# Moving the second attention's exp into a step of its own, and spreading the first attention's reciprocals half by half

## The chip, the cores and the metric

The kernel runs on one NeuronCore of one Trainium2 chip. The metric is the device time of one execution in microseconds. Before the change three runs took 3222.53, 3224.51 and 3226.42 us, with a median of 3224.51 us. The profile comes from another execution of the same program, which took 3221.87 us; the span of its instructions is 3220.1 us.

## The reference

Two layers on an image batch `x` of shape (2, 256, 64, 64), all in 32-bit floats.

Layer 0 is full attention over the 4096 pixels of each image, with 8 heads of 32 channels, followed by a 1x1 convolution and a blend by a resized mask:

```python
q = proj(Wq, bq) / math.sqrt(hd); k = proj(Wk, bk); v = proj(Wv, bv)
attn = softmax(einsum('bnd,bmd->bnm', q, k), axis=-1)
fuse = einsum('bnm,bmd->bnd', attn, v)
hybrid = conv1x1(concatenate([x, fuse], axis=1), Wf, bf)
x = hybrid * m + x * (1.0 - m)
```

Layer 1 has a channel gate, attention inside windows of 8 x 8 pixels with 4 heads of 64 channels, and then two grouped 7 x 7 convolutions with normalisation, whose result gates `x`:

```python
x = x * sigmoid(relu(xp @ ca_w1 + ca_b1) @ ca_w2 + ca_b2)
attn = softmax(einsum('whqd,whkd->whqk', q, k) * hd ** (-0.5), axis=-1)   # second attention
o = einsum('whqk,whkd->whqd', attn, v) @ out_w + out_b
x = x + o; x = channel shuffle of x in 4 groups
y = bn2(conv7x7(relu(bn1(conv7x7(x, sa_w1) + sa_b1)), sa_w2) + sa_b2)
return x * sigmoid(y)
```

## The kernel before

A first part (about 210 us) computes queries, keys and values of layer 0 for both images, writes them to DRAM, and prepares the weights of the convolutions. It also decides whether the scores are small enough for a softmax without a shift; with the inputs used they are, and the version of the main part without the shift (its tiles have an `a` in the name) runs.

The main part is a pipeline of 1024 slots. A slot is one image `b` (2), one chunk `c` of 512 query pixels (8 per image), one group `g` of four heads (2), and one block `m` of 128 keys (32). So a pair (b, c) takes 64 slots. In this document the 16 pairs are chunks 0 to 15, and a slot's place inside its chunk is its position, 0 to 63; positions 0 to 31 are the first half (g = 0), 32 to 63 the second.

The order of instructions on every engine is written out by hand: no scheduler reorders them[...]. In slot i, the loop at the end of `pipeline` issues:

- `scores(i + 2)`: four matmuls (L593), one for each head on its own 32 rows of the array, into four PSUM banks, and the exp of these banks on ACT (L603) into an `e` tile. There are five `e` tiles in rotation (`EB = 5`).
- `products(i)`: four matmuls (L622) that add values times `e` into the accumulator `av`; and on DVE the running sum of the `e` tiles over the keys (L624, 128 x 2048 elements), from the half's second slot on. An `e` tile is free once both have read it.
- `run_later()`: the actions put off by `at(delay, action)`. At the end of each chunk these make the reciprocals of the softmax denominators: `denominators` (L645, on PE, reads the two running sums of the chunk), a reciprocal (L673, DVE), `spread` (L659, matmuls that copy each head's reciprocal to the 32 rows of its channels, and two copies L667 on ACT), and the multiplication of the attention's result `f` (L675, DVE). Seen from the next chunk these fall on positions 1, 2, 3 and 4.
- `run_stages()`, in every fourth slot: one step of the generator `stage(b, c)`, which does everything from the 1x1 convolution of layer 0 to the output of the second attention for the chunk before. Its steps end at each `yield`. At positions 8, 12, ..., 52 it issues: the 1x1 convolution `hy` (L693), the two matmuls of the channel gate (L722, L736), queries and keys of the second attention (L762, two steps), its values (L780), the step with its scores (L799) and softmax (L807 to L811), the row sums and division (L814 to L816), the transposes (L824), the products (L837), the output projection (L857), and the addition into `xo` (L868) with its stores `xs` (L883).
- `run_convs()`, in every fourth slot two slots later: one step of `convolve`, which does the two convolutions of an image once its last stage is through: in turn conv1 (L936), conv2 (L959) and gate with the output stores (L981, L990). Image 0's convolution runs beside chunks 8 to 11; image 1's runs after all slots.

[...] One is the accumulator's. While no convolution is under way, the others form two pairs (`psum2`) and three single banks (`psum1`); a slot's scores take one pair and two singles. While one is under way, there are three pairs and one single, and a slot's scores take two pairs. Denominators, spread, stages and conv2 take pairs from the same rotation, conv1 takes a single. A pair is given out again when its last reader is done.

In the step with the second attention's scores and softmax, the queue order is: matmuls on PE; a copy from PSUM on ACT (L807); maximum (L809) and subtraction (L810) on DVE; exp on ACT (L811). It falls on position 32, the first slot of a half, which has no running sum.

Of the kernel before, what the change touches and what calls it, by code (L numbers as in the profile page):

```python
# [19 lines left out]
P = 128  # L20
KC = C // P
# [32 lines left out]
def conv_seq_kernel(ctx: ExitStack, tc: tile.TileContext, a, out):  # L54
    nc = tc.nc
# [13 lines left out]
    def psum2(name):  # L69
        return ps["pair"].tile([P, 2, CH], F32, tag="s", name=name)  # L70
# [41 lines left out]
    for u in range(4):  # L112
        t = const.tile([P, len(BLOCKS), UG, WP], F32, name=f"xc{u}")
        nc.gpsimd.memset(t, 0.0)
        xcs.append(t)
        t = const.tile([P, UQ, len(BLOCKS), WP], F32, name=f"yc{u}")
# [77 lines left out]
    with (  # L194
# [9 lines left out]
        for n in ("bq", "bk"):  # L204
            t = w0.tile([P, KC], F32, name=n)
# [8 lines left out]
        for b in range(B):  # L214
            src = a["x"][b].rearrange("(k p) h w -> p k (h w)", p=P)
            for c in range(NCHUNK):
# [3 lines left out]
                for n, w in (("q", wq), ("k", wk)):  # L220
# [13 lines left out]
                    t = st0.tile([P, KC, CH], F32, tag=n, name=f"{n}st_{b}_{c}")  # L234
# [37 lines left out]
                i = b * NCHUNK + c  # L272
# [36 lines left out]
    def batch_norm(name, t):  # L309
        g, beta, mean, var, cbias = (t[:, :, i] for i in range(5))  # L310
        sc, sh = (cwp.tile(list(g.shape), F32, name=name + i) for i in ("_sc", "_sh"))
        nc.vector.tensor_scalar_add(sc, var, EPS)
        nc.scalar.activation(sc, sc, AF.Sqrt)
        nc.vector.reciprocal(sc, sc)
        nc.vector.tensor_mul(sc, sc, g)
        nc.vector.tensor_sub(sh, cbias, mean)
        nc.vector.tensor_mul(sh, sh, sc)
        nc.vector.tensor_add(sh, sh, beta)
        return sc, sh
# [30 lines left out]
    _, shj = batch_norm("bj", bj)  # L350
# [65 lines left out]
    def spread(row, n):  # L416
        f = row.shape[-1]
        return row.rearrange("p u f -> u p f").to_broadcast([NU, n, f])
# [58 lines left out]
    def pipeline(arm, shifted, pools):  # L477
# [6 lines left out]
        def psum_for(convolving):  # L484
            if convolving != few[0]:
                few[0] = convolving
                name = f"{arm}{now[0]}"
                psum_layout(name, *((3, 1) if convolving else (2, 3)))
# [12 lines left out]
        stages = deque()  # L501
# [3 lines left out]
        def at(delay, action):  # L505
            later.append((now[0] + delay, action))

        def load_piece(n):
            if n * PB >= len(slots):
                return  # L510
            b, c, g, m = slots[n * PB]
            p = m // PB
            nm_ = f"{arm}_{b}_{c}_{g}_{p}"
            k = kvp.tile([P, PB * P], F32, tag="k", name=f"k{nm_}")
            nc.sync.dma_start(k, k_s[b, g, p])
            v = kvp.tile([P, PB, P], F32, tag="v", name=f"v{nm_}")
            nc.sync.dma_start(v, v_s[b, g, p].rearrange("p (m d) -> p m d", m=PB))
            kts[b, c, g, p], vts[b, c, g, p] = k, v

        def load_q(b, c):  # L520
            q = qp.tile([P, KC, CH], F32, tag="q", name=f"q{arm}_{b}_{c}")
            nc.sync.dma_start(q, q_s[b, c].rearrange("p (g n) -> p g n", g=KC))
            qts[b, c] = q
# [87 lines left out]
        def products(i):  # L611
            b, c, g, m = slots[i]
            if m == 0:
                acc[0] = avp.tile([P, CH], F32, tag="av", name=f"av{arm}_{i}")
                acc[1] = ep.tile([P, HG, CH], F32, tag="sum", name=f"sum{arm}_{i}", bufs=3)
                totals[b, c, g] = acc[1]
            av, total = acc[0], acc[1]
            e, v = es[i], vts[b, c, g, m // PB]
            start, stop = m == 0, m == NMB - 1
            for j in range(HG):  # L620
                r = slice(32 * j, 32 * j + 32)
                nc.tensor.matmul(av[r, :], v[:, m % PB, r], e[:, j, :], start=start, stop=stop)  # L622
            if m > 0:
                nc.vector.tensor_add(total, first[0] if m == 1 else total, e)  # L624
            e = es.pop(i)
            if start:
                first[0] = e
            if stop:
                if g == 0:
                    fts[b, c] = fp.tile([P, KC, CH], F32, tag="f", name=f"f{arm}_{b}_{c}")  # L630
                f = fts[b, c]
                nc.scalar.copy(f[:, g, :], av)  # L632
                if g == 0:
                    return
                both = [totals.pop((b, c, gg)) for gg in range(KC)]
                inv = fp.tile([P, P], F32, tag="inv", name=f"inv{arm}_{i}")
                rd = fp.tile([P, KC, 4, P], F32, tag="rd", name=f"rd{arm}_{i}")


                def denominators():  # L640
                    s = psum2(f"dn{arm}_{i}")
                    for h in range(HEADS0):
                        for q in range(4):
                            r = slice(32 * q, 32 * q + 32)
                            nc.tensor.matmul(  # L645
                                s[r, 0, 0:P],
                                keysum[:, h].rearrange("p i h -> p (i h)"),
                                both[h // HG][:, h % HG, q * P : (q + 1) * P],
                                start=(h == 0),
                                stop=(h == HEADS0 - 1),  # L650
                            )
                    nc.scalar.copy(inv, s[:, 0, 0:P])

                def spread():
                    tiles = [psum2(f"rd{arm}_{i}_{hh}") for hh in range(2)]
                    for gg in range(KC):
                        for q in range(4):
                            r = slice(32 * q, 32 * q + 32)
                            nc.tensor.matmul(  # L659
                                tiles[q // 2][:, q % 2, gg * P : gg * P + P],  # L660
                                spread_h[r, gg].rearrange("p j d -> p (j d)"),
                                inv[r, :],
                                start=True,
                                stop=True,
                            )
                    for hh in range(2):
                        nc.scalar.copy(  # L667
                            rd[:, :, 2 * hh : 2 * hh + 2, :],
                            tiles[hh][:, :, 0 : KC * P].rearrange("p q (g n) -> p g q n", g=KC),
                        )  # L670

                at(2, denominators)
                at(3, lambda: nc.vector.reciprocal(inv, inv))  # L673
                at(4, spread)
                at(5, lambda: nc.vector.tensor_mul(f, f, rd.rearrange("p g q n -> p g (q n)")))  # L675


        def stage(b, c):
            x, f = xts.pop((b, c)), fts.pop((b, c))
# [8 lines left out]
            t = gp.tile([P, KC, CH], F32, tag="t", name=f"t{tag}")  # L688
# [44 lines left out]
            for oc in range(KC):  # L733
                for h in range(2):
                    r = slice(64 * h, 64 * h + 64)
# [7 lines left out]
            t = gp.tile([P, KC, CH], F32, tag="t", name=f"sg{tag}")  # L743
# [13 lines left out]
            for h in range(2):  # L757
# [11 lines left out]
                for j in range(KC):  # L769
                    n = 2 * h + j  # L770
# [21 lines left out]
            for hc in range(2):  # L792
                for t in range(4):
                    for w in range(2):
                        for h in range(2):
                            r = slice(64 * h, 64 * h + 64)
# [11 lines left out]
            mx = gp.tile([P, 16], F32, tag="mxw", name=f"mxw{tag}")  # L808
            nc.vector.tensor_reduce(mx, e, AX.X, ALU.max)  # L809
            nc.vector.tensor_sub(e, e, mx.unsqueeze(2).to_broadcast([P, 16, 64]))  # L810
            nc.scalar.activation(e, e, AF.Exp, scale=HD1**-0.5)  # L811
            yield
            rs = gp.tile([P, 16], F32, tag="rsw", name=f"rsw{tag}")
# [7 lines left out]
            for n in range(16):  # L821
                for w in range(2):
                    r = slice(64 * w, 64 * w + 64)
# [7 lines left out]
            for hc in range(2):  # L831
                for t in range(4):
                    for w in range(2):
                        for h in range(2):
                            n = 2 * hc + h
                            r = slice(64 * w, 64 * w + 64)
# [30 lines left out]
            for oc in range(KC):  # L867
# [5 lines left out]
                for n, (x0, _, _) in enumerate(BLOCKS):  # L873
# [4 lines left out]
                    for h in range(2):  # L878
                        q = 2 * oc + h
                        p = 32 * q + 1 - x0  # L880
# [135 lines left out]
        def run_later():  # L1016
            for _ in range(len(later)):
                due, action = later.popleft()
                if due <= now[0]:
                    action()  # L1020
                else:
                    later.append((due, action))
# [15 lines left out]
        for i, (b, c, g, m) in enumerate(slots):  # L1038
            now[0] = i
            psum_for(bool(convs))  # L1040
            if m % PB == 0:
                load_piece(i // PB + AHEAD)
            if g == KC - 1 and m == 0:
                nxt = (b, c + 1) if c + 1 < NCHUNK else (b + 1, 0)
                if nxt[0] < B:
                    load_q(*nxt)
            rest = scores(i + 2) if i + 2 < len(slots) else None
            products(i)
            if rest:
                rest()  # L1050
            if g == KC - 1 and m == NMB - 1:
                at(6, lambda b=b, c=c: stages.append(stage(b, c)))
            run_later()
            if i % 2:
                next(banded, None)
            if i % 4 == 0:
                run_stages()
            if i % 4 == 2:
                run_convs()
# [94 lines left out]
```

## Time and profile before

| engine | busy, us | share of the span |
|---|---|---|
| PE (matmul) | 3110.8 | 97% |
| DVE | 2553.6 | 79% |
| ACT | 2377.1 | 74% |
| POOL | 400.9 | 12% |

| part of a plain slot | time, us |
|---|---|
| L593, eight matmul records together | 1.14 |
| L622, eight matmul records together | 1.06 |
| L603, the exps of four banks | about 2.0 |
| L624, running sum | 2.29 |

An engine's share of busy time is an average over the whole span. A matmul of 32-bit floats leaves two records in the profile, and the records of matmuls on different rows of the array overlap. In lists of waits, the engine that waits is on the left and what ended the wait on the right, followed by the total in us, how often, and the longest. In the timeline a line is a start, a duration, the engine, the source line and the tiles; in square brackets stands the idle time of that engine just before, with what ended it. In tables of stretches each engine has its busy time and, in brackets, its number of instructions; PEclk is the clock granted to PE as a share of the full one.

### The profile page before, as it was taken

What the parts mean: (1) busy time and instruction counts of PE and PEld (TensorE: products, weight loads), DVE (VectorE), ACT (ScalarE), POOL (GpSimd) and SP (SyncE); (2) the same over time, 40 slices, a digit from 0 to 9 for tenths busy, and PEclk for the clock granted to TensorE, in tenths of its full rate; (3) what the DMA queues carried; (4) which work ended last, traced back from release to release, by engine and by line L of the source; (5) the groups of instructions that cost most, each with busy time, mean ns of one, the idle gap of its engine ahead of it and who ended that gap; (6) DMA issues with size and microseconds to landing.
All of it is one profiled execution on the core that took longest, in us unless ns stands there. A gap on an engine that the chain in (4) does not pass through costs nothing. (4 is left out here: it accounts for less than half of the span.)

```text
span 3220.1 us, 62227 instructions
## 1 busy us (share of the span) xinstructions
PE 3110.8 (97%) x26122; PEld 1097.9 (34%) x26122; DVE 2553.6 (79%) x1388; ACT 2377.1 (74%) x3432; POOL 400.9 (12%) x693
## 2 busy tenths in 40 slices
PE   9989999999999999999999999999999999999868
PEld 4532322222232322222233434444332222222257
DVE  3349888898989989898987787777788988888711
ACT  2359788897878787888877676776778888888623
POOL 8121002020200000000000121121200000000015
PEclk9999999999999999999999999999999999999989
DMA  7965115252433131221213232232321213121335
GB/s 212 345 144 74 60 55 67 66 66 65 73 66 69 56 74 58 66 66 54 73 54 112 88 105 91 87 91 81 80 63 57 76 53 76 53 66 58 111 91 162
DMA packets 156258, 278.96 MB, mean 87 GB/s; under 512 B 36520, under 2 KB 55708, under 8 KB 155968
## 3 DMA queue, kind: packets, MB, share of 16 engines
q1 hardware_dynamic: 126496, 234.30, 24.1%
q0 software_dynamic: 25504, 38.02, 8.0%
q8 instruction: 207, 3.39, 0.4%
q10 hardware_dynamic: 3968, 2.57, 0.3%
q14 instruction: 83, 0.68, 0.1%
HBM read 212.57 MB, written 65.21 MB: 86 GB/s over the span
## 5 line engine op out<-in xcount | busy, mean ns | idle before, releaser
L624 DVE TENSOR_TENSOR suma<-suma,ea 128x2048 f32<-128x2048 f32 x960 | 2198.7, 2290 | 153.8 <-ACT ea L603 71.5
L603 ACT ACTIVATE ea<-sa 128x512 f32<-128x512 f32 (+1 forms) x2866 | 2032.0, 784 | 154.2 <-PE sa L593 95.8
L593 PE MATMUL sa<-qa,ka 32*128 32x512 f32 x8192 | 1261.5, 647 | 43.9 <-ACT ea L603 36.0
L622 PE MATMUL ava<-ea,va 128*32 128x512 f32 x8192 | 1107.6, 613 | 0.5 <-ACT fa L632 0.5
L593 PEld LDWEIGHTS sa<-qa,ka 32*128 32x128 f32 x8192 | 367.9, 185 | 844.5 <-ACT ea L603 641.2
L622 PEld LDWEIGHTS ava<-ea,va 128*32 128x32 f32 x8192 | 162.5, 108 | 795.1 <-issue 769.0
L883 POOL DMA_DIRECT2D xs<-xo x94 | 66.0, 709 | 2025.0 <-DVE xo L868 2024.3
L990 POOL DMA_DIRECT2D out_dram<-za x288 | 161.1, 569 | 562.8 <-ACT ea L603 305.4
L762 PE MATMUL qka<-ua,qkv_w 128*128 128x512 f32 x256 | 121.0, 617 | 2.6 <-DVE ua L754 2.6
L959 PE MATMUL c2a<-yc,wa 32*128 32x192 f32 x1792 | 115.6, 401 | 0.1
L959 PEld LDWEIGHTS c2a<-yc,wa 32*128 32x128 f32 x1792 | 107.8, 321 | 18.8 <-ACT ea L603 12.6
L981 DVE TENSOR_TENSOR za<-za,xc 128x768 f32<-128x768 f32 x32 | 30.5, 954 | 98.0 <-ACT za L975 67.6
L771 ACT ACTIVATE qka<-qka,qkv_b 128x512 f32<-128x512 f32 x64 | 40.5, 684 | 90.5 <-PE qka L762 90.5
L705 DVE TENSOR_TENSOR ta<-ta,mca 128x512 f32<-128x512 f32 x32 | 22.0, 688 | 98.8 <-ACT ta L701 98.8
L809 DVE TENSOR_REDUCE mxwa<-ewa 128x16 f32<-128x1024 f32 x16 | 19.5, 1220 | 100.2 <-ACT ewa L807 100.2
L969 ACT ACTIVATE za<-c2a 128x384 f32<-128x384 f32 x64 | 28.0, 488 | 94.4 <-PE c2a L959 60.4
L936 PE MATMUL c1a<-xc,wa 128*32 128x192 f32 x1792 | 82.8, 334 | 14.2 <-DMA xc<-xs 12.6
L701 ACT ACTIVATE ta<-hya,bf 128x512 f32<-128x512 f32 x32 | 20.2, 683 | 100.1 <-PE hya L693 93.9
L624 DVE TENSOR_TENSOR suma<-ea,ea 128x2048 f32<-128x2048 f32 x32 | 73.1, 2286 | 25.6 <-DMA va<-vs 13.5
L936 PEld LDWEIGHTS c1a<-xc,wa 128*32 128x32 f32 x1792 | 71.5, 139 | 29.7 <-issue 26.1
L239 ACT ACTIVATE qsq<-q,bq 128x512 f32<-128x512 f32 x32 | 22.0, 687 | 78.1 <-DVE qst L238 78.1
L436 POOL DMA_DIRECT2D ws<-r2s x112 | 69.4, 622 | 67.4 <-DMA ws<-r2s 33.1
(137 smaller groups left out, 1609.6 us busy)
## 6 DMA issues: line engine op xcount, KB each, us to landing
ka<-ks SPq DMA_DIRECT2D x256, 256.0 KB
va<-vs SPq DMA_DIRECT2D x256, 256.0 KB
wa<-ws SPq DMA_DIRECT2D x32, 896.0 KB
ws<-zero POOLq DMA_DIRECT2D x16, 896.0 KB, 21.8
xc<-xs SPq DMA_DIRECT2D x32, 420.0 KB
xs<-xo POOLq DMA_DIRECT2D x78, 140.0 KB, 7.2
x<-in_x_dram SPq DMA_DIRECT2D x16, 512.0 KB
ks<-kst SPq DMA_DIRECT2D x32, 256.0 KB
```

The costliest lines, as they stand in the source:

```text
L436: nc.gpsimd.dma_start(band2[:, at0 : at0 + step * (n - 1) + 1 : step, :], spread(r2_s[k : k + 1, :, i], n),)
L593: nc.tensor.matmul(heads[j], k[r, cols], q[r, g, :], start=True, stop=not shifted)
L603: nc.scalar.activation(e[:, h, :], tile, AF.Exp, scale=SCALE0)
L622: nc.tensor.matmul(av[r, :], v[:, m % PB, r], e[:, j, :], start=start, stop=stop)
L624: nc.vector.tensor_add(total, first[0] if m == 1 else total, e)
L762: nc.tensor.matmul(s[:, j, :], wqkv[:, kc, o : o + P], u[:, kc, :], start=(kc == 0), stop=(kc == KC - 1),)
L771: nc.scalar.activation(qk[:, n, :], s[:, j, :], AF.Identity, bias=bqkv[:, n : n + 1], scale=0.5)
L883: eng.dma_start(x_s[b][n, p + r0 : p + r1].rearrange("r g w -> g r w"), xo[64 * h : 64 * h + 64, oc, r0 - WS * c : r1 - WS * c, :],)
L936: nc.tensor.matmul(s[32 * j : 32 * j + 32, q, 0 : nb * W], w[:, 4 * q + j, d, :], x[:, 0:nb, 4 * q + j, d : d + W], start=(d == 0), stop=( ...
L959: nc.tensor.matmul(tiles[j // 2][:, j % 2, q * nb * W : (q + 1) * nb * W], w[r, q, d], y[r, q, 0:nb, d : d + W], start=(d == 0), stop=(d = ...
L981: nc.vector.tensor_mul(z, z, x[:, 0:nb, :, PAD : PAD + W].rearrange("p n g x -> p g n x"))
L990: eng.dma_start(dst[i, r0:r1, UG * u : UG * u + UG, :], z[p + r0 : p + r1, :, n, :])
```

## The change

Three edits.

- `stage` gets a `yield` between the subtraction and the exp. The exp (L811) is now issued by the stage's next step, four slots later, and so is every step after it: row sums, transposes, products, projection and the addition with its stores now fall on positions 40, 44, 48, 52 and 56.
- `spread` now takes an argument `hh` and handles half of the tokens (two of the four blocks of 128 pixels): one pair of banks, the matmuls of two blocks of rows for both groups of heads, and one copy. It is called in two successive slots (delay 4 and 5), and the multiplication of `f` moves to delay 6. Before, one call took two pairs, ran all matmuls with the head group as the outer loop, and then made both copies.
- The stage of a chunk joins the list of stages after a delay of 7 slots, not 6.

```diff
-                def spread():
-                    tiles = [psum2(f"rd{arm}_{i}_{hh}") for hh in range(2)]
+                def spread(hh):
+                    t = psum2(f"rd{arm}_{i}_{hh}")
                     for gg in range(KC):
-                        for q in range(4):
-                            r = slice(32 * q, 32 * q + 32)
+                        for q in range(2):
+                            r = slice(64 * hh + 32 * q, 64 * hh + 32 * q + 32)
                             nc.tensor.matmul(
-                                tiles[q // 2][:, q % 2, gg * P : gg * P + P],
+                                t[:, q, gg * P : gg * P + P],
                                 spread_h[r, gg].rearrange("p j d -> p (j d)"),
                                 inv[r, :],
...
-                    for hh in range(2):
-                        nc.scalar.copy(
-                            rd[:, :, 2 * hh : 2 * hh + 2, :],
-                            tiles[hh][:, :, 0 : KC * P].rearrange("p q (g n) -> p g q n", g=KC),
-                        )
+                    nc.scalar.copy(
+                        rd[:, :, 2 * hh : 2 * hh + 2, :],
+                        t[:, :, 0 : KC * P].rearrange("p q (g n) -> p g q n", g=KC),
+                    )
...
-                at(4, spread)
-                at(5, lambda: nc.vector.tensor_mul(f, f, rd.rearrange("p g q n -> p g (q n)")))
+                at(4, lambda: spread(0))
+                at(5, lambda: spread(1))
+                at(6, lambda: nc.vector.tensor_mul(f, f, rd.rearrange("p g q n -> p g (q n)")))
...
             nc.vector.tensor_sub(e, e, mx.unsqueeze(2).to_broadcast([P, 16, 64]))
+            yield
             nc.scalar.activation(e, e, AF.Exp, scale=HD1**-0.5)
...
-                at(6, lambda b=b, c=c: stages.append(stage(b, c)))
+                at(7, lambda b=b, c=c: stages.append(stage(b, c)))
```

## The prediction

> **What bounds the kernel now.** I read the page first, then the waits, then the timeline around one spot where the change acts, then stretches. The page:
>
> ```profile
> PE 3110.8 (97%) x26122; PEld 1097.9 (34%) x26122; DVE 2553.6 (79%) x1388; ACT 2377.1 (74%) x3432; POOL 400.9 (12%) x693
> L624 DVE TENSOR_TENSOR suma<-suma,ea 128x2048 f32<-128x2048 f32 x960 | 2198.7, 2290 | 153.8 <-ACT ea L603 71.5
> ```
>
> PE looks like the bound, DVE like an engine with a fifth to spare. Both are averages. A slot without extra work takes PE 2.07 us (distance between the first L622 matmuls of two slots in the timeline), while the running sum L624 takes DVE 2.29 us, in 31 of 32 slots. In plain slots DVE is the slower of the two; PE falls back only where a stage or convolution step gives it more. The waits:
>
> ```profile
> ACT ewa L811 <- DVE ewa L810: 41.8, 16, 2.6
> PE sa L593 <- ACT ea L603: 36.0, 20, 2.4
> DVE mxwa L809 <- ACT ewa L807: 100.2, 16, 15.7
> PE dna L645 <- DVE suma L624: 8.4, 5, 5.5
> ACT ea L603 <- DVE suma L624: 15.4, 36, 0.8
> ```
>
> In each of 16 chunks the second softmax's exp (L811) sits on ACT for 2.6 us until DVE has done maximum and subtraction; the first attention's exps queue behind it and PE runs out of banks. One such spot (chunk 13, positions 32 to 35), timeline of DVE, ACT and PE:
>
> ```profile
> 2616.70 1.22 DVE L809 TENSOR_REDUCE mxwa<-ewa 128x16 f32<-128x1024 f32 x1 [5.13 <-ACT ewa L807]
> 2618.02 1.23 DVE L810 TENSOR_TENSOR ewa<-ewa,mxwa 128x1024 f32<-128x1024 f32 x1
> 2619.28 1.06 ACT L811 ACTIVATE ewa<-ewa 128x1024 f32<-128x1024 f32 x1 [2.61 <-DVE ewa L810]
> 2620.88 2.07 PE L593 MATMUL sa<-qa,ka 32*128 32x512 f32 x2 [2.17 <-ACT ea L603]
> 2622.88 1.94 PE L622 MATMUL ava<-ea,va 128*32 128x512 f32 x8
> 2624.74 2.09 PE L593 MATMUL sa<-qa,ka 32*128 32x512 f32 x8
> 2626.76 1.47 PE L622 MATMUL ava<-ea,va 128*32 128x512 f32 x8
> 2628.16 1.14 PE L593 MATMUL sa<-qa,ka 32*128 32x512 f32 x8
> ```
>
> PE stands 2.17 us and then runs at about half rate (1.94 for eight L622 records, else 1.06). Slots 32 to 35 take 15.82 us; slots 44 to 47, with an equal PE step (64 small matmuls), take 9.37: a loss of 6.45 us. The stretches, the third of them being everything DVE does from L809 to the chunk's last sum:
>
> ```profile
> core 0: us, PE busy (x) PEld busy (x) DVE busy (x) ACT busy (x) POOL busy (x), PEclk, DMA share, GB/s
> 2616.60:2629.20 12.60, 10.43 (x52) 2.16 (x48) 12.15 (x7) 6.91 (x11) 0.00 (x0) 0.73 0.09 23
> 2529.40:2616.70 87.30, 86.96 (x648) 26.46 (x648) 74.21 (x38) 70.36 (x107) 0.00 (x0) 1.00 0.19 61
> 2616.70:2697.10 80.40, 78.23 (x668) 20.63 (x669) 77.03 (x39) 69.29 (x105) 5.71 (x8) 0.96 0.30 67
> 1844.00:1935.00 91.00, 88.64 (x894) 35.45 (x896) 78.92 (x41) 66.59 (x76) 22.89 (x40) 0.98 0.31 94
> ```
>
> The reader should see that DVE is busy throughout PE's stall (12.15 of 12.60), and for 77.03 of 80.40 us to the end; the rest is the 0.10 us between two DVE instructions in a row. The second half of this chunk is already DVE's, stall or no stall; the first half is PE's (86.96 of 87.30). With the convolution running (last line) both have room on DVE.
>
> [...]the exps of L603 stand behind L811 for its 2.61 us. [...]here a 2.17 us gap is enough (granted clock 0.73 over the stall's stretch), and gaps of 1.2 us (chunk 1's denominators) are not. [...]the spread's 16 records (four row groups) take 0.90 us in chunk 9, against 0.27 each.
>
> **Part by part.**
>
> 1. Exp a step later. L811's 2.61 us wait goes: at position 36 its input is long ready. Its 1.06 us on ACT stays; it moves to a slot without other ACT work, where ACT has 2.0 us per slot against DVE's 2.40, so it is hidden by DVE's lag; with convolution I allow 0.3 us each. The sums, products, transposes, outputs and the DMAs of xs move from 36, 40, ... 52 to 40, ... 56, with the same neighbours; POOL's xs stores (8 per chunk) are not waited for before the convolution, which starts one step later too. The last stage runs after all slots, with nothing between: nothing there.
>
> 2. Chunks without convolution (1 to 8, 12 to 15). From the start of L809 to the end of the last L624 DVE's timeline gives 80.05 us where it never waits (chunks 6, 12), otherwise up to 80.56. All of that work stays in the same half. Removable: the excess over 80.05 (0.53, 0.43, 0.43, 0.38, 0.36, 0.02, 0.17, 0.42, 0.02, 0.37, 0.43, 0.43), in sum 4.0. Then the denominators wait for the last sum: the next slot's L622 begins 2.67 us after it in most chunks, 2.14 where PE already waits; I take 2.18. That frees 0.49 six times, about nothing in four, and 5.36 in chunk 8, where conv1(0) fell: in sum 8.3. So 12.3 us, not 12 x 6.45. PE's remaining gain turns into small waits for e buffers, which DVE frees. Chunk 0 has no stage and shows this end state already: 2.40 us per slot, ACT waiting 0.39 per slot for L624, a gap of 1.19 us at the denominators, full clock after it.
>
> 3. Chunks 9 to 11, with convolution. Here DVE is idle 9 to 11 us beyond its small gaps and PE is the bound. Slots 32 to 35 against 44 to 47 with the same convolution step: 14.91 against a nominal 9.86, 15.60 against 12.15, 19.68 against 13.94; stalls of 5.05, 3.45, 5.74, together 14.2. Less 3 x 0.3 for the moved exp, less 2.3 because every convolution step is four slots later and conv1(0) (a slot of 4.38 instead of 2.07) moves from chunk 8, which DVE bounds, into chunk 9. Net 11.0.
>
> 4. The spread. It took both pairs of banks in one slot: the second waits for an exp (the records split, 0.65 us apart) and the next scores for the copies. Slots 3 and 4 take 3.98 + 2.07. New: the same 16 records, 8 per slot, two row groups at a time. Unknown price: 0.9 us in all if the records overlap as now, 1.8 if two groups halve the rate; I take 1.3. Then 2 x 2.07 + 1.3 = 5.44, a gain of 0.6 in eleven chunks; in chunks 9 to 12, which have three pairs (3.63 + 2.07 in chunk 9), about nothing, with 0.4 for chunk 12. Sum 7.0. This half is PE's, so it counts. Copies (0.59 each) and L675 (1.22) fall one slot later; hy needs f at position 8, after a start of L675 at about 5 to 6: hidden. In the tail the first copy overlaps the second half's matmuls: 0.4.
>
> 5. The stage's start at delay 7: position 6 instead of 5, but stages run only where the position divides by four, so at 8 as before. Nothing.
>
> Sum: 12.3 + 11.0 + 7.0 + 0.4 = 30.7. Span 3220.1 - 30.7 = 3189.4. The profiled run took 3221.87 and the runs' median is 3224.51, 4.4 above the span: 3194.
>
> **Rivals.**
>
> - PE really is the bound and all stalls come back: 12 x 6.4 = 77, with 11 and 7 about 95, so 3130. For it: 97% and the chain of waits, which is mostly PE. Against: 31 sums at 2.396 and seven other operations fill 80 us, and nothing takes any away. 0.05.
> - The stall's disappearance helps DVE or the convolution more than counted (L624 waits less in chunks 9 to 11, or the spread's whole 0.75 and a shorter denominator wait): 10 to 15 us more, 3180. 0.15.
> - The wait moves. At position 40 the row sums put 2.8 us on a DVE that now lags further, exp(46) is held, PE idles at 44 and cools once more; the transposes there (2.0 us of PE) cover most, and PE has about 5 us to spare in that half. If it happens in most chunks, items 2 and half of 3 go: 3212. 0.12.
> - Slower: PE, arriving early, stands at the denominators (position 1) for over 2 us and cools just as the PE-bound half begins. Price 6.45 - 2.17 = 4.3 us in each of eleven chunks, 47 against 30.7: 3240. It decides from the seventh such chunk on. Against it stands chunk 0's end, the same state with 1.19 us idle and a full clock. 0.07.
> - The change does little: the spread with two row groups costs 1.8 us and more and the convolution's stalls are replaced by waits for pairs of banks: 12 left, 3213 or above. 0.05.
>
> The rest, 0.56, is my forecast, 3194 with 3184 to 3206 as its own range. Two runs of this kernel differ by up to 0.12%, so 0.2% (6.4 us) is about what can be told from no change. For 8 in 10 I leave out the first rival and the slow one, and some of the ends of the others: 3174 to 3214. Faster by over 0.2%: all but the slow case, and part of the third and fifth: 0.86. Within 0.2%: 0.06. Slower: 0.08.
>
> **What would show it.** L811's wait on L810 is gone, L593's waits on L603 with 2.2 us gone. L603's wait for L624 (15.4 us now) grows to over 60 us, and the denominators' wait for L624 (now 5 times, the longest 5.5 us in the tail) appears in about twelve chunks. From L809 to the last L624 it is 80.0 to 80.1 us in chunks without convolution. Slots 33 to 35 of chunks 9 to 11 lose 3 to 6 us each. Slots 3 and 4 take about 2.7 each. Wrong would be: a second half shorter than 80 us from L809 (then DVE did not bound it), PEclk under 1.00 in a first half, or half-rate L622 after the denominators.

## The result and the profile after

The changed kernel takes 3194.58 us (median of four runs, 3193.36 to 3198.20); the kernel before takes 3224.45 us (four runs). The ratio is 0.9909, with a 95% interval of 0.9892 to 0.9926: 0.9% faster, 29.9 us by the medians. The profiled execution has a span of 3193.9 us against 3220.1.

First the page after, the same two lines as before, and the group of L593:

```profile
PE 3100.5 (97%) x26122; PEld 1116.1 (35%) x26122; DVE 2553.6 (80%) x1388; ACT 2368.8 (74%) x3432; POOL 401.0 (13%) x693
L624 DVE TENSOR_TENSOR suma<-suma,ea 128x2048 f32<-128x2048 f32 x960 | 2198.9, 2291 | 145.6 <-ACT ea L603 60.3
L593 PE MATMUL sa<-qa,ka 32*128 32x512 f32 x8192 | 1269.4, 640 | 12.8 <-DMA va<-vs 7.7 <-ACT ea L603 5.1
```

The busy shares have hardly moved; 97% of PE says nothing of what happened. The waits do (who waited, for what: total us, times, longest):

```profile
ACT ea L603 <- DVE suma L624: 95.0, 168, 2.7
PE dna L645 <- DVE suma L624: 20.7, 13, 8.0
PE sa L593 <- ACT ea L603: 5.1, 14, 1.1
DVE mxwa L810 <- ACT ewa L808: 100.3, 16, 15.8
```

PE's standing for ACT's exps fell from 36.0 to 5.1 us. What came in its place is a queue behind DVE: ACT waits 95.0 us (15.4 before) for an `e` tile that the running sum has not yet released, and the denominators wait for the last sum 13 times instead of 5. DVE's wait for the second attention's scores, the line with L810, is as it was (100.2 before).

The spot shown before, now (chunk 13, timeline of DVE and ACT, and then PE at the next chunk's position 1):

```profile
2593.78 1.22 DVE L810 TENSOR_REDUCE mxwa<-ewa 128x16 f32<-128x1024 f32 x1 [5.13 <-ACT ewa L808]
2595.11 1.23 DVE L811 TENSOR_TENSOR ewa<-ewa,mxwa 128x1024 f32<-128x1024 f32 x1
2602.36 1.10 ACT L813 ACTIVATE ewa<-ewa 128x1024 f32<-128x1024 f32 x1
...
2672.09 1.06 PE L645 MATMUL dna<-suma,keysum 128*32 128x128 f32 x32
2674.25 1.08 PE L645 MATMUL dna<-suma,keysum 128*32 128x128 f32 x32 [1.10 <-DVE suma L624]
2675.26 1.14 PE L593 MATMUL sa<-qa,ka 32*128 32x512 f32 x8
2676.33 1.06 PE L622 MATMUL ava<-ea,va 128*32 128x512 f32 x8
```

The exp (now L813) starts without a wait. PE passes position 33 at full rate, and stands 1.10 us at the denominators instead, with a full clock after it. The stretches: around the old stall, all that DVE does from the maximum to the chunk's last sum, the first half before it, and chunk 9 with the convolution beside it:

```profile
2593.00:2606.00 13.00, 13.00 (x96) 3.08 (x88) 11.77 (x7) 12.12 (x19) 0.00 (x0) 1.00 0.20 63
2593.78:2674.19 80.41, 78.56 (x688) 22.68 (x685) 77.04 (x39) 69.83 (x106) 5.72 (x8) 1.00 0.29 70
2506.90:2593.70 86.80, 86.46 (x648) 26.57 (x647) 74.23 (x38) 70.20 (x107) 0.00 (x0) 1.00 0.20 61
1830.50:1920.50 90.00, 90.00 (x910) 36.63 (x910) 79.47 (x41) 68.84 (x78) 17.71 (x31) 1.00 0.33 97
```

PE is now busy for all of the first stretch, with the full clock (1.00, against 0.73 around the stall before). Yet the second one is 80.41 us long where it was 80.40: counted from the maximum, the end of DVE's work in this chunk moved by nothing at all, although PE lost a stall of 6.45 us.

### The profile page after: what moved, and what is told of

It is laid out like the page before. It is cut to its first block, busy times and chain, and to the rows that moved or that the text cites. A ratio compares the mean times of both kernels' runs of the same rounds, so it can differ in the third digit from the quotient of the medians.

```text
span 3193.9 us, 62245 instructions
## 1 busy us (share of the span) xinstructions
PE 3100.5 (97%) x26122; PEld 1116.1 (35%) x26122; DVE 2553.6 (80%) x1388; ACT 2368.8 (74%) x3432; POOL 401.0 (13%) x693
## 3 DMA queue, kind: packets, MB, share of 16 engines
q8 instruction: 207, 3.39, 0.4%
## 4 chain that ended last, share of the span: by engine, by line
PE 64%; DVE 21%; issue 5%; ACT 3%; DMA 1%; POOL 0%; DVEq 0%; SPq 0%; ACTq 0%; POOLq 0%
PE sa L593 24%; PE ava L622 21%; DVE suma L624 19%; PE qka L763 3%; PE hya L694 3%; PE c2a L961 3%; PE c1a L938 2%; ACT ea L603 2%; PE vwa L781 2%; PE opa L859 2%; PE rda L660 1%; PE ca2a L737 1%; PE oa L839 0%; PE ca1a L723 0%; PE pta L826 0%
## 5 line engine op out<-in xcount | busy, mean ns | idle before, releaser
L624 DVE TENSOR_TENSOR suma<-suma,ea 128x2048 f32<-128x2048 f32 x960 | 2198.9, 2291 | 145.6 <-ACT ea L603 60.3
L593 PE MATMUL sa<-qa,ka 32*128 32x512 f32 x8192 | 1269.4, 640 | 12.8 <-DMA va<-vs 7.7
L622 PE MATMUL ava<-ea,va 128*32 128x512 f32 x8192 | 1091.6, 605 | 3.3 <-ACT fa L632 3.3
L593 PEld LDWEIGHTS sa<-qa,ka 32*128 32x128 f32 x8192 | 387.4, 183 | 786.5 <-ACT ea L603 575.6
L622 PEld LDWEIGHTS ava<-ea,va 128*32 128x32 f32 x8192 | 161.5, 108 | 782.0 <-issue 752.6
L810 DVE TENSOR_REDUCE mxwa<-ewa 128x16 f32<-128x1024 f32 x16 | 19.5, 1220 | 100.3 <-ACT ewa L808 100.3
L938 PE MATMUL c1a<-xc,wa 128*32 128x192 f32 x1792 | 82.5, 334 | 13.5 <-DMA xc<-xs 12.9
L624 DVE TENSOR_TENSOR suma<-ea,ea 128x2048 f32<-128x2048 f32 x32 | 73.1, 2285 | 21.5 <-DMA va<-vs 13.4
```

Of the source, the lines that this page charges most:

```text
L593: nc.tensor.matmul(heads[j], k[r, cols], q[r, g, :], start=True, stop=not shifted)
L938: nc.tensor.matmul(s[32 * j : 32 * j + 32, q, 0 : nb * W], w[:, 4 * q + j, d, :], x[:, 0:nb, 4 * q + j, d : d + W], start=(d == 0), stop=( ...
```

## The experiments

All times are medians; a ratio is that to the kernel before, run on the same chip beside the experiment, with its 95% interval. The experiments ran in four batches, in which the kernel before took 3223.5 to 3230.1 us; so where two versions of different batches are compared, the difference of the ratios stands beside that of the medians if the two differ much.

**One part alone.** The `yield` without the spread:

```diff
             nc.vector.tensor_sub(e, e, mx.unsqueeze(2).to_broadcast([P, 16, 64]))
+            yield
             nc.scalar.activation(e, e, AF.Exp, scale=HD1**-0.5)
```

> The exp in a step of its own, the spread left as before. DVE-bound theory: of the 12 chunks without convolution only the slack of DVE's second half comes back (about 1 us each), the convolution's chunks 9 to 11 and chunk 8's end give the rest; about 3201 us, 23 below before; from the maximum L809 to the chunk's last sum 80.0 to 80.4 us in the 12 chunks. PE-bound rival: every stall of 6.4 us comes back, about 3140 us.

3205.19 us, ratio 0.9934 (0.9921 to 0.9947): 19.7 us below before, where 23 were expected. From the maximum to the last sum it is 80.05 to 80.42 us in the 12 chunks, as expected of a DVE bound. The rival's 3140 us is far away.

The spread without the `yield`:

> The spread by halves in two slots, the exp left behind the subtraction in one step. Theory: the first half of the 12 chunks without convolution is PE's, so the about 0.45 us per chunk that slots 3 and 4 lose counts in full, with half a us in the tail: about 3218 us, 6 below before; the 2.2 us gaps of PE at position 33 stay. Rival (the two parts only work together): no change, 3224 us.

3216.84 us, ratio 0.9976 (0.9965 to 0.9986): 8.0 us below. The stall is untouched, as its wait line shows (36.0 us before):

```profile
PE sa L593 <- ACT ea L603: 35.4, 17, 2.4
```

The parts add up, 19.7 + 8.0 against 29.9 together, within what the runs can tell. The 8.0 us rest on the median of ten runs: in this kernel's trace the stall costs 4.9 us in some chunks and 6.5 in others, and that moves the length of a chunk more than the spread does. Beside the exp's step, where no stall blurs it, the first half of a regular chunk takes 91.2 us with the old spread and 90.8 with the new one: 0.4 us per chunk.

**Is DVE the second half's bound?** Both kernels without the row sums, reciprocal and division of the second attention:

```diff
-            rs = gp.tile([P, 16], F32, tag="rsw", name=f"rsw{tag}")
-            nc.vector.tensor_reduce(rs, e, AX.X, ALU.add)
-            nc.vector.reciprocal(rs, rs)
-            nc.vector.tensor_mul(e, e, rs.unsqueeze(2).to_broadcast([P, 16, 64]))
```

> The changed kernel without the row sums, reciprocal and division of the second attention (left out, so that DVE has 2.7 us less work in each second half; PE's and ACT's instructions stay). DVE-bound theory: each of the 12 second halves without convolution gets 2.8 us shorter, about 34 us in all: 3161 us. PE-bound rival: PE issues the same matmuls, so 3195 us.

> The kernel before without the same row sums, reciprocal and division. Theory of two near-equal bounds: PE's stall holds the second half at nearly the same length as DVE does, so taking DVE's 2.7 us away gives only the half us of denominator wait in a few chunks: 3220 to 3224 us. If DVE alone had bounded the kernel before: about 3190 us.

From the changed kernel it takes 3172.15 us, 22.4 below it (ratio to before 0.9841, 0.9823 to 0.9859); by the profiled spans 3167.6 against 3193.9, 26.3 us. From the maximum to the last sum it is now 77.57 to 77.94 us, 2.48 less in each chunk, so I had the removed work 0.3 us too dear. Twelve times 2.48 would be 29.8 us; in the profiled run PE waited for pieces of keys and values in chunks 0 and 4 and lost 3.2 us again. PE's matmuls were all still there: the time left with DVE's work, which refutes the PE bound. In the stretch of chunk 13:

```profile
2574.89:2652.82 77.93, 76.61 (x688) 21.66 (x684) 74.53 (x36) 70.20 (x106) 5.73 (x8) 1.00 0.32 72
```

From the kernel before, the same removal gives 3216.68 us, ratio 0.9971 (0.9957 to 0.9985), 8 us where 1 to 5 were expected. In five of the twelve chunks without convolution (2, 3 and 13 to 15) it stays at 80.2 to 80.5 us from the maximum to the last sum, with DVE now idle for up to 2.9 us of it: there PE's stall alone holds it. In three (1, 4 and 12) it is 78.8 to 78.9, and in four (5 to 8) 77.6 to 77.9 us. In these four the stall came and the clock did not fall (chunk 6):

```profile
1307.19 1.12 PE L593 MATMUL sa<-qa,ka 32*128 32x512 f32 x2 [2.17 <-ACT ea L603]
1308.24 1.06 PE L622 MATMUL ava<-ea,va 128*32 128x512 f32 x8
```

The gap is 2.17 us, to the hundredth that of the prediction's example, and the eight L622 records after it take 1.06 us, not 1.94. The granted clocks of that stretch and of chunk 13's in the same run:

```profile
1303.00:1316.00 13.00, 10.83 (x80) 2.52 (x78) 12.54 (x7) 10.28 (x16) 0.00 (x0) 1.00 0.19 46
2606.60:2620.00 13.40, 11.23 (x60) 2.31 (x56) 12.66 (x7) 7.78 (x13) 0.00 (x0) 0.75 0.14 37
```

By the prediction's own measure (slots 32 to 35 less slots 44 to 47) the stall costs 3.3 us in these four chunks: 2.17 of standing, and 1.1 because the last two of the eight L593 records now run by themselves (1.12 us for the two, where all eight together take 1.14). In the other eight chunks it costs 4.8 to 5.0 or 6.3 to 6.5 us. So half clock adds nothing, about 1.6 or about 3.2 us, and which of these does not depend on the gap's length alone. The times of the sixteen runs say the same of the whole kernel: they spread from 3201.53 us, with a mean granted clock of 0.983, to 3229.18, with 0.974. What else it depends on, no run here shows.

**Shifting work from the half that PE bounds to the half that DVE bounds.** If the second half is DVE's and the first PE's, PE steps should move from the first to the second. The stage is begun later, by its delay alone:

```diff
-                at(7, lambda b=b, c=c: stages.append(stage(b, c)))
+                at(11, lambda b=b, c=c: stages.append(stage(b, c)))
```

> The changed kernel with every stage begun four slots later (delay 11), so that the values' step (3.65 us of PE) moves from the first half of a chunk, which PE bounds, into the second, which DVE bounds, and DVE no longer waits at a half's start for the second attention's scores. Theory: 3.65 us of PE and about 2.8 us of DVE waiting go from the longest path of each of the 12 chunks without convolution, until PE's own sum (163 us of 169) is the bound: 5 us each, about 3138 us (3130 to 3155). Rival (PE at 97% is the bound throughout, and has the same matmuls): 3195 us.

3180.04 us, ratio 0.9863 (0.9846 to 0.9879): 14.5 us below the changed kernel, where about 57 were expected. The first half got shorter as expected (87.4 us from first L622 to first L622, 90.8 before), but DVE lost most of it again. Its timeline in chunk 13:

```profile
2583.05 4.69 DVE L624 TENSOR_TENSOR suma<-suma,ea 128x2048 f32<-128x2048 f32 x2 [2.67 <-ACT ea L603]
2590.40 1.22 DVE L810 TENSOR_REDUCE mxwa<-ewa 128x16 f32<-128x1024 f32 x1 [2.66 <-ACT ewa L808]
```

DVE caught up during the values' step and stood 2.67 us for want of an `e` tile (scores run two slots ahead, no further), and 2.66 us more for the second attention's scores. I had taken it that a DVE bound means that DVE finds work; it does only while it lags.

With eight slots (`at(15, ...)`), and with the spread later as well (delays 3, 4, 6, 7, 8 for denominators, reciprocal, both halves of the spread and the multiplication):

> The same with the stage eight slots later (delay 15): one step of queries and keys moves across too. Theory: PE's sum bounds both halves, so about as the one with four slots, 3135 us. Rival (PE-bound before already): 3195 us.

> The stage eight slots later, and denominators, reciprocal, spread and the multiplication moved one to two slots later (delays 3, 4, 6, 7, 8), so that PE does not wait there for DVE's last sum (1.1 us) and reciprocal (0.34 us). Theory: up to 1.4 us for each of 12 chunks below the one with eight slots if DVE still lags there, nothing if it has caught up: 3120 to 3135 us. Rival: 3195 us.

3165.72 us (0.9815, 0.9798 to 0.9831) and 3160.42 us (0.9801, 0.9785 to 0.9817). Both beat the changed kernel, the rival of 3195 us is wrong, and both are above what I expected: a chunk takes 166.1 us in the second of them, not the 163 of PE's own sum. The spread's later place gives 5.3 us by the medians, at the edge of what the intervals separate.

The stage four slots later with the exp left behind the subtraction (the changed spread stays):

> As the first of these, but with the exp left right behind the subtraction, in one step. Theory: with the stall of 4 to 6 us per chunk in place PE's sum is 168 to 169 us per chunk, so the later stage brings little: 3200 to 3217 us, and the exp's own step is then worth 60 to 75 us, not the 21 that it is worth with DVE as a second bound. Rival (the exp's step is worth about 21 us wherever the stage stands): 3160 us.

3202.07 us, ratio 0.9930 (0.9913 to 0.9946), inside the expected range; but since the kernel with the exp's step came only to 3180.04, the step is worth 22.0 us here and 22.3 us with the stage in its old place. That is what the rival said of the step (about 21 us wherever the stage stands), though not the time that it gave (3160). My expectation of 60 to 75 us fell with that of the stage's place.

**DVE's own wait in the same step.** In the changed kernel DVE still stands 5.13 us ahead of L810, in order behind a maximum whose scores are not there yet. The change's remedy for ACT, applied to DVE:

```diff
             nc.scalar.copy(e, s.rearrange("p u (n k) -> p (u n) k", k=64))
+            yield
             mx = gp.tile([P, 16], F32, tag="mxw", name=f"mxw{tag}")
             nc.vector.tensor_reduce(mx, e, AX.X, ALU.max)
```

> The changed kernel with one more step boundary: between ACT's copy of the second attention's scores and DVE's maximum, so that DVE no longer stands at position 32 until the scores are there, but goes on with the running sums. Theory: DVE's second half then begins with the sum at position 33 about 2.8 us earlier, with the same work; 2.8 us in each of 12 chunks: 3162 us. Rival (those 5 us of DVE idle time are idle for want of e tiles anyway): 3195 us.

3176.34 us, ratio 0.9831 (0.9814 to 0.9849): 18 us below the changed kernel by the medians, 25 by the ratios, 33 expected; the rival's 3195 is wrong. The mechanism is the expected one. DVE goes on with the sums, and meets the maximum four slots later without a wait:

```profile
2586.82 2.29 DVE L624 TENSOR_TENSOR suma<-ea,ea 128x2048 f32<-128x2048 f32 x1 [2.33 <-ACT ea L603]
2589.21 7.09 DVE L624 TENSOR_TENSOR suma<-suma,ea 128x2048 f32<-128x2048 f32 x3
2596.22 1.21 DVE L811 TENSOR_REDUCE mxwa<-ewa 128x16 f32<-128x1024 f32 x1
2597.47 1.22 DVE L812 TENSOR_TENSOR ewa<-ewa,mxwa 128x1024 f32<-128x1024 f32 x1
```

A regular chunk takes 166.1 us instead of 169.3, 3.2 less, a little more than expected. The rest was lost in chunks 2 to 4, whose first halves grew from 90.8 to 94.7, 97.5 and 102.7 us. There PE waits for a piece of keys, as it does for up to 3.5 us in seven of the earlier traces, though not in that of the changed kernel. The issues on SP's queue in chunk 4 are slow at that place (the median issue of a key piece takes 0.32 us), and two queues have stood long before:

```profile
PE sa L593 <- DMA ka<-ks: 15.6, 4, 8.6
SPq L528 <- DVE x1a L708: 185.0, 15, 12.5
POOL xs L886 <- DVE xo L871: 1961.0, 16, 235.9
...
904.89 0.38 SPq L528 DMA_DIRECT2D xa<-in_x_dram  x1
905.33 0.46 SPq L531 DMA_DIRECT2D mca<-masks  x1
905.88 5.22 SPq L515 DMA_DIRECT2D ka<-ks  x1
911.20 4.22 SPq L517 DMA_DIRECT2D va<-vs  x1
```

The stage's load of the next x (L528) waits on SP's queue until DVE has read the last one, about 12.4 us in each of 15 chunks, with the next key and value pieces behind it. In most chunks PE never stands for it. In chunks 2 to 4 the issues that follow are slow as well, here 5.22 us for the key piece; in these chunks, and in no later one, POOL's queue issues 8 to 10 transfers of the bands (the convolution's weights) in the 15 us after the load. They come there because the bands of a chunk stand behind the stores `xs` on POOL's queue and go out in one burst when `xo` is ready: at the end of chunk 3 POOL stood 123.27 us for `xo`, issued the eight stores in 5.52 us, and then the bands. With the further boundary that is four slots later, and the burst in chunk 2 reaches position 17, past the load of x at position 10; in the changed kernel it ends at position 9. That bands make the issues slow is read from this coincidence; it was not tested alone.

**Putting these together.** The further boundary with the later stage and spread, and with the later spread alone (delay 9 for the stage, so that it still starts at position 8):

> The same further step boundary in the kernel with the stage eight slots and the spread one to two slots later. Theory: DVE's wait for the scores goes here too, 2 to 3 us in each of 12 chunks, until PE's sum of 163 us bounds: about 3130 us. Rival: 3160 us, as without it.

> The further step boundary with the spread one to two slots later, and the stage where it was (position 8). Theory: as with the boundary alone less up to 1.4 us of PE waits in each of 12 chunks: 3145 to 3162 us; the stage's place is then worth what this lies above the one with the stage eight slots later. Rival: 3195 us.

3159.85 us (0.9782, 0.9765 to 0.9798) and 3169.71 us (0.9811, 0.9793 to 0.9829). The first was expected at 3130; its regular chunks take 164.6 us (166.1 without the boundary), but its first halves in chunks 2 to 4 take 92.9, 89.0 and 94.5 us against 85.4 later, with waits of 1.8 to 6.6 us for key pieces. Below the kernel that has all this but the boundary (3160.42) it is only 0.6 us by the medians and 6 by the ratios, so the rival's 3160 us, as without it, came out as a time. The second lies above its expected range. Its first halves in chunks 2 and 3 lost 4.3 and 4.6 us with key pieces, and in the regular ones PE's wait only moved: it no longer stands at the denominators, but for 0.76 us at position 8, where the stage needs the multiplied `f`, and 90.7 us are left of 91.1:

```profile
PE hya L694 <- DVE fa L676: 8.4, 11, 0.8
```

So, last, the transfers that may get in the way:

```diff
-            if i % 2:
+            if i % 2 and not 10 <= i % 64 < 26:
                 next(banded, None)
```

> The kernel with the maximum's step boundary, the stage eight slots later and the spread later, with one thing more: the band transfers on POOL's queue are not issued at positions 10 to 25, around the stage's load of x and mask at position 16. Theory: in chunks 2 to 4 PE stood up to 6.6 us (15.2 in all) for a key piece whose load on SP's queue was held up behind x and mask while the bands were under way[...]; those first halves take 92.9, 89.0 and 94.5 us, later ones 85.4, so about 20 us go: 3140 us. Rival (key pieces are late because of x and mask alone): 3160 us, as without the pause.

3146.34 us, ratio 0.9755 (0.9737 to 0.9772): the fastest version, 2.4% below the kernel before, and 13.5 us below the one without the pause by the medians, 9 by the ratios (whose intervals still overlap); 20 were expected. Chunk 2's first half is back to 85.4 us; chunks 3 and 4 still take 88.0 and 92.7. Chunk 3 has a wait of 2.5 us for a piece of values at position 16, and chunk 4 this one:

```profile
PE sa L593 <- DMA ka<-ks: 4.3, 1, 4.3
```

So the bands share in the delay. In chunk 2, where POOL's last band now goes out at position 16, ahead of the load of x at 18, it is gone. But the bands are only put off, and POOL's queue lags behind the slots: in chunk 4 it still issued bands up to position 20, and the key piece there took 6.44 us to issue. A queue of its own for the stores, or for x and mask, was not tried.

## Why the prediction was right

The forecast was 3194, the result 3194.58. Part of that is luck: the terms were off by a few us, and offset by the runs' spread.

1. That DVE bounds the second half of chunks without convolution, and would turn a PE gain of 6.45 us into about 1: right, and shown. From L810 to the last L624 it is 80.05 to 80.06 us in eight of the twelve chunks and 80.35 to 80.41 in chunks 1, 3, 5 and 13, where a gap of 0.46 us stands ahead of one L624 (no wait that the trace names explains it, and it stays open). Chunk 13 before had such a gap too, so "the rest" of its 80.40 us was not only the 0.10 us between instructions: these make 2.9 of the 3.37. And each excess in the prediction's list is 0.02 too large; over 80.05 they sum to 3.75, not 4.0. The next slot's L622 begins 2.13 or 2.14 us after the last sum throughout, against an assumed 2.18. The two experiments without the row sums and the one with the maximum's own step show the bound, not only the lengths.

2. By stretches, from chunk 1's position 2 on: up to the last sum of chunk 8 the gain is 7.2 us where the terms gave 9.5 (the spread's 0.16 too much in eight chunks and the gaps of 0.46 that stand in three make the difference); from there to that of chunk 12, with the convolution, 16.3 against 16.8; to that of chunk 15, 3.1 against 4.0; in the tail 0.6 against 0.4. In all 27.2 against 30.7; the profiled run of the changed kernel was 1.04 us behind when it came to chunk 1, so the spans differ by 26.2. The medians differ by 29.9: that the forecast met the result to 1 us is the luck.

3. The term that was mis-sized is the spread: slots 3 and 4 take 2.91 + 2.70 = 5.61 us against 6.05 before, a gain of 0.44 per chunk, not 0.6. Slot 3 has a 0.34 us wait of L660 for the reciprocal that I had not counted. The choice of 1.3 us for the records on two row groups was near: with that wait taken off it is 5.27 - 4.14 = 1.1.

4. The exp's 1.06 us in its new slot: 1.10 us, without a wait ahead of it in 15 of 16 chunks (2.6 us in the tail). PE's slot 37 grows from 2.07 to 2.66 us, hidden by DVE's lag as assumed.

5. Convolution: slots 33 to 35 of chunks 9 to 11 take 26.0 us together, 40.1 before. The single chunks are not alike, since each slot has another step of the convolution now: in chunk 9 slot 33 fell from 5.80 to 2.07 us, but slot 34 grew from 3.39 to 6.21, so that chunk lost 1 us where 3 to 6 were named as a sign. PE is busy through all 90 us of the stretch shown.

6. Rivals: the PE bound was refuted by the exp's step alone (3205, not 3140). The half clock at the denominators (the slow rival) did not come: 1.10 us of standing in all such chunks and a full clock behind it (granted clock 1.00 from 230 to 3008 us), as at chunk 0's end. The second fall to half clock, at position 44, did not come either: PE stands 0.2 to 0.6 us there, after the transposes (2.08 us in chunk 13) have covered the rest. The rivals of 3180 us (more comes back) and of 3213 and above (little does) lie outside the changed kernel's four runs.

The pricing of the stall itself was a single chunk's. In the profile that the prediction read, the same measure gives 6.25 to 6.55 us in nine of the twelve chunks, but 4.9 in chunks 5, 6 and 12, in sum 73 and not 77; and the same gap cost 3.3 us in four chunks of an experiment. Had PE been the only bound, the forecast would have leaned on it.

## What to carry to other kernels

Before counting the time that a removed stall gives back, add up the other engines' work over the same stretch: here DVE had 80.05 us to do in 80.5, so a PE stall of 6.45 us was worth one. Average shares (97% and 79%) hide that two halves of one loop body have different bounds; a table of stretches shows it. And an instruction that waits with others behind it in its engine's queue is worth a step of its own on every engine that it blocks: the exp on ACT (2.61 us in chunk 13) and the maximum on DVE (5.13 us) were two such cases (a gain of 20 us from the kernel before, and of 18 from the changed one), and the load of x on SP's queue (up to 12.5 us) and the stores on POOL's (up to 235.9 us) may be others. Gains of such edits do not simply add: the kernel with the later stage and spread is 34 us below the changed one, and the maximum's step on top of it brought nothing that is clear of noise.

## What the runs showed of the hardware that I had not expected

- A TensorE gap of about 2.2 us was followed by half clock in some chunks (eight L622 records in 1.94 us) and by the full clock in others (1.06 us), within one execution. In the four traces that have the stall, its cost in the 48 chunks without convolution falls into three groups: 3.2 to 3.3 us (5 chunks), 4.8 to 5.0 (19) and 6.2 to 6.6 (24). In the kernel before the granted clock was 0.50 for 6.83 us in each of the nine chunks of the highest group (from 2620.80 us in chunk 13) and for 3.41 us in chunks 5, 6 and 12, and 1.00 again after it. By estimate from 1.94 against 1.06 us for the same records, 3.41 us of half clock cost 1.5 us, about the steps of 1.6 us between the groups.
- The issue of one 256 KB load on SP's queue took 5.22 us, and that of the next 4.22, right behind a load of x and mask while the bands were issued from POOL's queue; the median is 0.32 us.
